# A planned graph-network kernel: transfers planned to land later, and the first filter taps and six filter steps moved ahead of the first transposition

## The chip, the cores and the metric

The kernel runs on one core of a Trainium2 chip. The metric is the device time of one execution in microseconds (us); lower is better. A core has TensorE (PE in the profile: matmuls, with the weight loads in a row of their own, PEld), VectorE (DVE), ScalarE (ACT), GpSimd (POOL) and SyncE (SP). Each works through its own queue in order. SP, ACT and POOL also issue transfers (DMAs).

## The reference

For 64 graphs of 256 nodes with 256 channels, one layer is computed: a layer norm with relu, then three branches (a convolution of width 1 and one of 17 taps along the nodes, a message step over an affinity matrix masked by the adjacency, and a gated recurrent cell that joins them), and a residual.

```python
h = jnp.maximum(_layernorm(x, axis=-1), 0.0)
xc = jnp.transpose(h, (0, 2, 1))
c = relu(bn1(conv1d(xc, conv1_w, 0)))
c = bn2(conv1d(c, conv2_w, 8))                       # 17 taps
x_conv = jnp.transpose(relu(c + xc), (0, 2, 1))
s = h @ w_se.T + b_se                                # 3 numbers a node
A = jnp.exp(-dist(s)) * adj
x_nmp = A @ relu(h @ w_msg.T + b_msg)
gi = jnp.concatenate([x_conv, x_nmp], -1) @ w_ih.T + b_ih
gh = h @ w_hh.T + b_hh
r, z = sigmoid(gi_r + gh_r), sigmoid(gi_z + gh_z)
n = tanh(gi_n + r * gh_n)
out = x + (1 - z) * n + z * h
```

## The kernel before, in words

The 64 graphs go in pairs (32 pairs, index i), and four pairs form a block (index b, 8 blocks). The 17-tap convolution is done in a transformed domain, a hand-written Fourier transform over 16 points on DVE (class Fft), so that the convolution becomes matmuls with transformed filters.

The filters are made once, at the start: `load_taps` brings the raw taps of some groups of channels (a group is 7 channels by 17 taps, 119 rows) into the tile taps, `load_points` the fixed matrices of points, and `filters` runs two matmuls aux<-taps,points or acc<-taps,points (256 columns each), one eviction by ACT (Yv<-aux, or taps<-acc where it overwrites the taps) and one transfer filt<-Yv or filt<-taps to memory. `filter_steps(n)` takes the next n of these from the list steps; they are strewn between other work, to fill TensorE. Later wb<-filt brings the filters back into the slots wb.

`norm` normalizes one pair in place: `stats` (DVE bn_stats st<-x, mv, rstd, a power on POOL), then DVE or ACT. The first four pairs lie in x, T, Sv and PT. `transpose_h` turns a pair by TensorE (aux<-ident,x) and evicts with relu into hT; `conv1` is the width-1 convolution; `split` feeds its output into V and U, the input of the transform. Before the first transposition TensorE runs WARM dummy matmuls on a zeroed tile (aux<-e).

From the second block on, a pair is turned by transfers: ACT writes hh, a transposing transfer makes halves, `sort_h` copies them back into hh, and `join_h` copies hh into hT by two ACT copies (hT<-hh). The adjacency goes the same way (`turn_adj`, `load_adj`, `join_adj`: adj<-adjh), and so does the output (`finish`, `deliver`: back<-tr, a transposing transfer gn<-back, back<-gn). x_rows holds one pair of x at a time; the next is loaded when the one before has been read by `turn_h`.

The gates of a pair are made by `seven`: a first product (acc or aux) is negated by ACT (acc<-acc) and evicted (wb<-aux), and later products are added by DVE (aux<-acc,wb and acc<-acc,wb). The sums of operand blocks that this needs are made by DVE (wb<-hT, wb<-xnm, wb<-Yv, `sums`).

The order on every engine is not that of the program. Each call is recorded as a Task, and `plan` orders the recorded tasks by a model: each engine takes, of the tasks that can start soonest, the one with the earliest late time. For TensorE late is its own running total of planned time; for a task that feeds TensorE it is worked back from there. pace is how far TensorE has come in that scale, and CALM (20 us) is the margin beyond which a task counts as not urgent. A transfer is modelled as one shared channel: self.dma is when the channel has moved it, and done, the time from which its readers can be planned, came 1.1 us later. On the chip the engines wait on semaphores, so a wrong guess of a landing costs a wait in the queue but not correctness.

`emit` is called twice. The first call comes in block 0, in front of `aggregate(0)`, and plans everything recorded by then (tasks from index 0); the second plans the rest (from a higher index), to the end. In `plan`, new is the range of the tasks that one call plans.

Of the kernel before, what the change touches and what calls it, by code (L numbers as in the profile page):

```python
# [249 lines left out]
class Recorder:  # L250
# [144 lines left out]
    def plan(self, fixed=False):  # L395

        T, new = self.tasks, range(self.planned, len(self.tasks))
        self.planned = len(T)
        total = 0.0
        for k in new:  # L400
            t = T[k]
            for p in t.preds:
                T[p].succs.append(k)
            if t.engine == "tensor":
                t.late = total
                total += t.cost
        for k in reversed(new):
            t = T[k]
            for s in t.succs:
                t.late = min(t.late, T[s].late - self.lag(t, T[s]) - self.cost(t))  # L410
            if t.first is not None:
                t.late = t.first - 1e6
        ready, free = {e: [] for e in self.LAG}, self.free
        left = {}

        def enable(k):
            at = max((T[p].done + self.lag(T[p], T[k]) for p in T[k].preds), default=0.0)
            ready[T[k].engine].append((at, k))
        for k in new:
            left[k] = sum(p in left for p in T[k].preds)  # L420
            if not left[k]:
                enable(k)
        order = []
        self.pace = 0.0

        def when(e, at, t):
            now = max(free[e], at)
            if t.size:
                now = max(now, self.lanes[e == "gpsimd"][0])
                if e != "gpsimd" and self.pace + self.CALM < t.late < math.inf:  # L430
                    now = max(now, self.dma - 1.0)
            return now

        def commit(k, e, at, now):
            t = T[k]
            ready[e].remove((at, k))
            t.begin = now
            free[e] = t.done = now + t.cost
            if e == "tensor":
                self.pace = max(self.pace, t.late)  # L440
            if t.size:
                if t.cost == self.TURN:
                    free[e] = max(free[e], self.dma + 1.1)
                self.dma = max(self.dma, now + 1.6) + t.size
                t.done = self.dma + 1.1
                lanes = self.lanes[e == "gpsimd"]
                lanes.popleft()
                lanes.append(t.done)
            order.append(k)
            for s in t.succs:  # L450
                left[s] -= 1
                if not left[s]:
                    enable(s)
        while fixed and len(order) < len(new):
            k = new[len(order)]
            e = T[k].engine
            at = next(at for at, j in ready[e] if j == k)
            commit(k, e, at, max(free[e], at, self.lanes[e == "gpsimd"][0] if T[k].size else 0.0))
        while len(order) < len(new):
            best = []  # L460
            for e in ready:
                cand = [(when(e, at, T[k]), T[k].late, k, at) for at, k in ready[e]]
                if cand:
                    now = min(cand)[0]
                    best.append((now, min(c[1:] for c in cand if c[0] <= now + 1e-9), e))
            now, (_, k, at), e = min(best)
            commit(k, e, at, now)
        return order
# [26 lines left out]
def kernel(  # L495
# [18 lines left out]
    nc = Recorder(tc.nc)  # L514
# [4 lines left out]
    PB = GB // G  # L519
    NB = B // GB  # L520
    NP = B // G
    DC = D // P
# [26 lines left out]
    def keep(name, *dims):  # L549
        return const.tile([P, *dims], FP, name=name)  # L550
# [24 lines left out]
    st, mv, rstd, shift = (Ring(keep(f"{name}{k}", *dims) for k in range(2)) for name, dims in (  # L575
        ("st", (G * MC, 6)), ("mv", (G * MC, 2)), ("rstd", (G * MC,)), ("shift", (G * MC,))))
    SLOTS = 9
    WARM = 21
    slots = [keep(f"wb{k}", DC, D) for k in range(SLOTS)]
    aux = Ring(psum.tile([P, W], FP, name=f"aux{k}") for k in range(4))  # L580
    acc = Ring(psum.tile([P, 2, W], FP, name=f"acc{k}") for k in range(2))
# [10 lines left out]
    PT, Sv, T = (Slots(t, GB * DC, L // 4, NW) for t in (PTt, Svt, Tt))  # L592
# [20 lines left out]
    def load_rows(t, src, i, eng, rows=rows):  # L613
        for g in range(G):
            eng.dma_start(out=row_tile(t, g), in_=rows(src, G * i + g))
# [4 lines left out]
    def load_x(i, eng=nc.sync):  # L620
        if i >= NP:
            return
        X[i] = SPARE[i].rearrange("p (q d) -> p q d", d=D) if i in SPARE else x_rows
        load_rows(X[i], x, i, eng, blocks if i <= PB else rows)
# [36 lines left out]
    NG = -(-P // KG)  # L661
    FULL = NG - 1
    MAIN = KG * TAPS // 16 * 16
    PARTS = [(0, FULL // 6), (FULL // 6, FULL // 3), (FULL // 3, FULL)]


    TURNS = []
# [14 lines left out]
    def load_taps(dc, a, b, eng):  # L682
        v = c2_wT[dc * P + a * KG:dc * P + b * KG].rearrange("(g k) t o -> (k t) g o", k=KG)
        for r in (slice(MAIN), slice(MAIN, KG * TAPS)):
            eng.dma_start(out=taps[r, a:b, dc, :], in_=v[r])
# [5 lines left out]
    def load_points(n, eng):  # L691
        f = bank_points[n]
        m = np.zeros((P, KG if n < len(PASSES) else LAST, f.shape[1]), np.float32)
        for k in range(m.shape[1]):
            m[k * TAPS:(k + 1) * TAPS, k] = f
        eng.dma_start(out=points[n], in_=tc.nc.inline_tensor(m.reshape(P, -1), name=f"points{n}").ap())
# [14 lines left out]
    nc.scalar.dma_start(out=w_c1, in_=c1_wT.rearrange("(k p) o -> p k o", p=P))  # L711
    load_vectors("bn1", bn1, nc.gpsimd)
    load_points(0, nc.scalar)
    for j in range(PB):
        load_x(j)
    for n in range(1, len(PASSES)):
        load_points(n, nc.sync)
    for dc in range(DC):
        load_taps(dc, *PARTS[0], nc.sync)
    load_points(len(PASSES), nc.sync)  # L720
    for part in PARTS[1:]:
        for dc in range(DC):
            load_taps(dc, *part, nc.sync)
    for dc in range(DC):
# [5 lines left out]
    p = aux()  # L730
    for _ in range(WARM):
        mm(p[:, :P], e_tile[:, 0, 0, :P], e_tile[:, 0, 0, :P], start=True, stop=True)
# [12 lines left out]
    def stats(i):  # L745

        if i >= NP:
            return
        s, m, r, h = STATS[i] = st(), mv(), rstd(), shift()
        for j in range(G * MC):  # L750
            nc.behind = BEHIND.get((i, j))
            nc.vector.bn_stats(s[:, j, :], X[i][:, j, :])
        nc.behind = None
        for j in range(G * MC):
            nc.vector.bn_aggr(m[:, j, :], s[:, j, :])
        nc.vector.tensor_scalar(r, m[:, :, 1], LN_EPS, None, ALU.add)
        if i < PB:
            BEHIND[i + 1, 0] = nc.last["vector"]
        nc.gpsimd.tensor_tensor(r, r, neg_half, ALU.pow)
        if i > PB:  # L760
            nc.vector.tensor_scalar(h, m[:, :, 0], -1.0, None, ALU.mult)
            nc.gpsimd.tensor_tensor(h, h, r, ALU.mult)
# [3 lines left out]
    def norm(i):  # L766
        stats(i)
        _, m, r, h = STATS[i]
        if i < PB:
            nc.vector.scalar_tensor_tensor(h, m[:, :, 0], -1.0, r, op0=ALU.mult, op1=ALU.mult)  # L770
        for j in range(G * MC):
            v = X[i][:, j, :]
            if i == PB or (i == 0 and j < MC):
                nc.vector.tensor_scalar(v, v, m[:, j, 0:1], r[:, j:j + 1], ALU.subtract, ALU.mult)
            else:
                nc.scalar.activation(v, v, AF.Identity, scale=r[:, j:j + 1], bias=h[:, j:j + 1])
        if i == 0:
            BEHIND[1, MC] = nc.last["vector"]
# [96 lines left out]
    def forward(k, kinds=(0, 1)):  # L875
        a = GB * DC // 2
        u, v, pt, sv, t = (s.among(k * a, (k + 1) * a) for s in (U, V, PT, Sv, T))
        if 0 in kinds:
            fft.odd(v, t, sv)
        if 1 in kinds:  # L880
            fft.even(u, pt, t)
# [413 lines left out]
            nc.gpsimd.dma_start(out=row_tile(y, g), in_=blocks(x, G * i + g), accum_op=ALU.add)  # L1295
            nc.gpsimd.dma_start(out=blocks(out, G * i + g), in_=row_tile(y, g))

    FIRST = PARTS[1][1]
    steps = deque((m, g) for g in range(FIRST) for m in range(len(PASSES)))
    steps.extend((0, g) for g in range(FIRST, FULL))  # L1300
    steps.append((len(PASSES), FULL))
    steps.extend((m, g) for m in range(1, len(PASSES)) for g in range(FIRST, FULL))
    banks = [0]

    def filter_steps(n, wide=True):
        for _ in range(n):
            banks[0] += 1
            p = acc()[:, 0] if wide and banks[0] % 3 == 0 else aux()
            filters(p, *steps.popleft(), nc.gpsimd if len(steps) % 2 else nc.sync)

    norm(0)
    power = nc.behind = nc.last["gpsimd"]
    nc.gpsimd.memset(h1, 0.0)
# [25 lines left out]
    for kind in (0, 1):  # L1339
        for k in range(2):  # L1340
            forward(k, (kind,))
    THIRD = FULL - FIRST
    filter_steps(len(steps) - THIRD - 8)
# [216 lines left out]
```

## Time and profile before

| | |
|---|---|
| median of three runs | 1669.88 us (1669.51 to 1676.13) |
| the profiled execution's own time | 1671.57 us |
| its span, first to last instruction | 1669.8 us |
| TensorE busy | 1652.6 us, 99% of the span |
| weight loads (PEld) busy | 1417.0 us, 85% |
| DVE busy | 1459.3 us, 87% |
| ACT busy | 1148.6 us, 69% |
| POOL busy | 242.5 us, 15% |
| mean granted TensorE clock | 0.997 of full speed |
| bytes moved by DMA | 261.39 MB, 157 GB/s on average |

The page sums busy time by engine. Beside it the trace gives each engine's timeline: start and duration of instructions in us, engine, output<-inputs, the shapes, the count in the row, and in brackets how long the engine had been idle and what released it. All instructions of the kernel carry the line of the helper that issues them (L378, or L374 for a joined group), so they are told apart by their tiles. A matmul in float32 shows as two records. Busy time of TensorE is modelled at its ends, so a slower stretch shows in the spacing of the starts rather than as idle time.

### The profile page before, as it was taken

The numbers are of one execution on the slowest core, as the hardware profiler recorded it, in microseconds if no ns is written. First come the engines' busy times: TensorE is split into PE (matmuls) and PEld (weight loads), VectorE is DVE, ScalarE is ACT, GpSimd is POOL, SyncE is SP. The second block draws the span as 40 slices with busy tenths as digits, with TensorE's granted clock in tenths as the row PEclk, the third lists the DMA queues.
The fourth block names the chain that finished last, engine by engine and source line by source line (L and its number), as shares of the span: only waits on it lengthen the run. The fifth ranks groups of instructions, "written<-read, shape, count | busy, mean of one in ns | idle before, by whom it ended". The sixth has DMA issues, their size and how long they took to land.

```text
span 1669.8 us, 26552 instructions
## 1 busy us (share of the span) xinstructions
PE 1652.6 (99%) x9008; PEld 1417.0 (85%) x9008; DVE 1459.3 (87%) x3391; ACT 1148.6 (69%) x2157; POOL 242.5 (15%) x245
## 2 busy tenths in 40 slices
PE   9999999999999999999999999999999999999999
PEld 6898778988899788988789887898889978898887
DVE  7979979899799997899888997989979899789645
ACT  5556676776767767686676777677676776667655
POOL 4211410013110131102110031001311013000010
PEclk9999999999999999999999999999999999999999
DMA  9982557846578455873568645784647835465022
GB/s 253 312 293 69 105 128 204 262 103 146 118 204 225 101 127 126 240 203 94 101 145 259 158 95 120 177 259 102 148 111 201 240 94 127 110 218 149 19 57 57
DMA packets 314938, 261.39 MB, mean 157 GB/s; under 512 B 192875, under 2 KB 240263, under 8 KB 314802
## 3 DMA queue, kind: packets, MB, share of 16 engines
q1 hardware_dynamic: 297010, 216.71, 49.1%
q0 software_dynamic: 17376, 42.66, 11.1%
q8 instruction: 71, 1.16, 0.3%
q14 instruction: 65, 0.53, 0.1%
q10 hardware_dynamic: 416, 0.32, 0.1%
HBM read 156.60 MB, written 43.78 MB: 120 GB/s over the span
## 4 chain that ended last, share of the span: by engine, by line
PE 79%; DVE 12%; DMA 4%; issue 2%; ACT 1%; SPq 1%; POOL 1%; ACTq 0%; DVEq 0%
PE acc L378 50%; PE aux L378 28%; DVE V L378 3%; DVE T L378 2%; DMA hh<-halves 2%; DVE Yv L378 2%; DVE wb L378 1%; DMA x<-in_x_dram 1%; PE aux L374 1%; DVE e L378 1%; SPq L378 1%; DMA wb<-filt 1%; POOL shift L378 1%; DVE msg L378 1%; DVE st L378 0%
## 5 line engine op out<-in xcount | busy, mean ns | idle before, releaser
L378 PE MATMUL acc<-wb,w_ih 128*128 128x256 f32 x768 | 189.9, 382 | 0.0
L378 PEld LDWEIGHTS acc<-wb,w_ih 128*128 128x128 f32 x768 | 146.0, 191 | 22.1 <-issue 2.3
L378 POOL DMA_DIRECT2D back<-in_x_dram x62 | 56.7, 1059 | 735.1 <-ACT back L378 594.1
L378 POOL TENSOR_TENSOR rstd<-rstd,neg_half 128x4 f32<-128x4 f32 x32 | 79.3, 2478 | 432.4 <-DVE shift L378 275.5
L378 DVE SCALAR_TENSOR_TENSOR V<-T,V 128x128 f32<-128x128 f32 (+2 forms) x448 | 141.5, 384 | 0.0
L378 ACT COPY back<-tr 128x512 uint16<-128x512 uint16 x124 | 130.4, 1078 | 15.7 <-DVE tr L378 15.3
L378 PE MATMUL aux<-wb,w_x 128*128 128x256 f32 x576 | 137.5, 381 | 2.6 <-DVE wb L378 2.6
L378 PE MATMUL acc<-wb,w_x 128*128 128x256 f32 x576 | 135.1, 380 | 0.0
L378 PEld LDWEIGHTS aux<-wb,w_x 128*128 128x128 f32 x576 | 108.7, 190 | 22.6 <-DVE wb L378 5.4
L378 PEld LDWEIGHTS acc<-wb,w_x 128*128 128x128 f32 x576 | 109.0, 190 | 18.6 <-issue 1.9
L378 PEld LDWEIGHTS acc<-U,wb 128*128 128x128 f32 x1024 | 118.3, 192 | 1.8 <-DMA wb<-filt 0.4
L378 PE MATMUL acc<-U,wb 128*128 128x128 f32 x1024 | 119.2, 275 | 0.3 <-DMA wb<-filt 0.3
L378 PE MATMUL aux<-w_msg,hT 128*128 128x259 f32 x512 | 118.6, 381 | 0.0
L378 PE MATMUL acc<-V,wb 128*128 128x128 f32 x1024 | 118.5, 275 | 0.0
L378 PEld LDWEIGHTS acc<-V,wb 128*128 128x128 f32 x1024 | 116.4, 192 | 0.5 <-DMA wb<-filt 0.5
L378 PE MATMUL acc<-wb,w_hh 128*128 128x256 f32 x384 | 105.7, 384 | 5.1 <-DVE acc L378 2.8
L378 DVE TENSOR_TENSOR e<-e,adj 128x256 f32<-128x256 f32 x128 | 68.7, 596 | 46.7 <-ACT e L378 46.7
L378 PEld LDWEIGHTS aux<-w_msg,hT 128*128 128x128 f32 x512 | 95.9, 190 | 14.1
L378 PE MATMUL aux<-hT,w_c 128*128 128x512 f32 x224 | 106.7, 600 | 0.3
L378 PE MATMUL acc<-Yv,w_ih 128*128 128x256 f32 x380 | 103.2, 381 | 2.1 <-ACT Yv L378 2.1
L378 PE MATMUL acc<-hT,w_hh 128*128 128x256 f32 x380 | 105.1, 383 | 0.0
L378 PE MATMUL acc<-xnm,w_ih 128*128 128x256 f32 x380 | 104.0, 380 | 0.0
(218 smaller groups left out, 3909.2 us busy)
## 6 DMA issues: line engine op xcount, KB each, us to landing
wb<-filt SPq DMA_DIRECT2D x348, 256.0 KB
back<-in_x_dram POOLq DMA_DIRECT2D x62, 256.0 KB, 5.3
out_dram<-back POOLq DMA_DIRECT2D x62, 256.0 KB, 3.1
x<-in_x_dram SPq DMA_DIRECT2D x58, 256.0 KB
halves_d<-halves SPq DMA_DIRECT2D x28, 512.0 KB
adjh<-halves_d SPq DMA_DIRECT2D x112, 128.0 KB
hh<-halves SPq DMA_DIRECT2D x108, 128.0 KB
filt<-Yv POOLq DMA_DIRECT2D x18, 224.0 KB, 4.3
```

What stands on the lines that cost most here:

```text
L374: self.tasks[k].call.append(lambda: method(*args, **kw))
L378: self.tasks.append(Task(engine, [lambda: method(*args, **kw)], cost, size, self.first))
```

## The change

In `plan`, `enable` sets when a task may start. A task that is not a transfer and has more than CALM to spare now gets, after each transfer that it reads, 3.0 us instead of the lag, which after a transfer is 0.0; in `commit`, a transfer's done is 2.1 us behind the channel instead of 1.1. Both are tied to new[0], the index of the first task that the call plans, being other than zero.

At the start, the first part of the taps, three groups, is split in two groups and one. The loads of the two groups stand directly behind the first pair of x, then the points, then the other three pairs of x, then the third group and the rest. The bound FIRST, the number of groups whose filter steps for all three passes come first, stays six, since its index into PARTS moves along. Six filter steps (two groups by three passes) are recorded ahead of `norm(0)`, and the dummy matmuls go from 21 to 16.

```diff
--- before.py
+++ after.py
@@ -414,7 +414,8 @@
         left = {}
 
         def enable(k):
-            at = max((T[p].done + self.lag(T[p], T[k]) for p in T[k].preds), default=0.0)
+            calm = 3.0 if new[0] and not T[k].size and self.pace + self.CALM < T[k].late < math.inf else 0.0
+            at = max((T[p].done + (calm if T[p].size else self.lag(T[p], T[k])) for p in T[k].preds), default=0.0)
             ready[T[k].engine].append((at, k))
         for k in new:
             left[k] = sum(p in left for p in T[k].preds)
@@ -442,7 +443,7 @@
                 if t.cost == self.TURN:
                     free[e] = max(free[e], self.dma + 1.1)
                 self.dma = max(self.dma, now + 1.6) + t.size
-                t.done = self.dma + 1.1
+                t.done = self.dma + (2.1 if new[0] else 1.1)
                 lanes = self.lanes[e == "gpsimd"]
                 lanes.popleft()
                 lanes.append(t.done)
@@ -575,7 +576,7 @@
     st, mv, rstd, shift = (Ring(keep(f"{name}{k}", *dims) for k in range(2)) for name, dims in (
         ("st", (G * MC, 6)), ("mv", (G * MC, 2)), ("rstd", (G * MC,)), ("shift", (G * MC,))))
     SLOTS = 9
-    WARM = 21
+    WARM = 16
     slots = [keep(f"wb{k}", DC, D) for k in range(SLOTS)]
     aux = Ring(psum.tile([P, W], FP, name=f"aux{k}") for k in range(4))
     acc = Ring(psum.tile([P, 2, W], FP, name=f"acc{k}") for k in range(2))
@@ -661,7 +662,7 @@
     NG = -(-P // KG)
     FULL = NG - 1
     MAIN = KG * TAPS // 16 * 16
-    PARTS = [(0, FULL // 6), (FULL // 6, FULL // 3), (FULL // 3, FULL)]
+    PARTS = [(0, 2), (2, FULL // 6), (FULL // 6, FULL // 3), (FULL // 3, FULL)]
 
 
     TURNS = []
@@ -711,14 +712,17 @@
     nc.scalar.dma_start(out=w_c1, in_=c1_wT.rearrange("(k p) o -> p k o", p=P))
     load_vectors("bn1", bn1, nc.gpsimd)
     load_points(0, nc.scalar)
-    for j in range(PB):
-        load_x(j)
+    load_x(0)
+    for dc in range(DC):
+        load_taps(dc, *PARTS[0], nc.sync)
     for n in range(1, len(PASSES)):
         load_points(n, nc.sync)
+    for j in range(1, PB):
+        load_x(j)
     for dc in range(DC):
-        load_taps(dc, *PARTS[0], nc.sync)
+        load_taps(dc, *PARTS[1], nc.sync)
     load_points(len(PASSES), nc.sync)
-    for part in PARTS[1:]:
+    for part in PARTS[2:]:
         for dc in range(DC):
             load_taps(dc, *part, nc.sync)
     for dc in range(DC):
@@ -1295,7 +1299,7 @@
             nc.gpsimd.dma_start(out=row_tile(y, g), in_=blocks(x, G * i + g), accum_op=ALU.add)
             nc.gpsimd.dma_start(out=blocks(out, G * i + g), in_=row_tile(y, g))
 
-    FIRST = PARTS[1][1]
+    FIRST = PARTS[2][1]
     steps = deque((m, g) for g in range(FIRST) for m in range(len(PASSES)))
     steps.extend((0, g) for g in range(FIRST, FULL))
     steps.append((len(PASSES), FULL))
@@ -1308,6 +1312,7 @@
             p = acc()[:, 0] if wide and banks[0] % 3 == 0 else aux()
             filters(p, *steps.popleft(), nc.gpsimd if len(steps) % 2 else nc.sync)
 
+    filter_steps(6)
     norm(0)
     power = nc.behind = nc.last["gpsimd"]
     nc.gpsimd.memset(h1, 0.0)
```

## The prediction

> **What bounds the kernel now.** I read the page's busy times first, then TensorE's own timeline for idle time, then the queues of ACT and DVE at each place where it stood idle, last the transfers.
>
> ```profile
> PE 1652.6 (99%) x9008; PEld 1417.0 (85%) x9008; DVE 1459.3 (87%) x3391; ACT 1148.6 (69%) x2157; POOL 242.5 (15%) x245
> ```
>
> PE is busy 99% of the span, so only three things can move the time: PE's dummy work at the start, its gaps, and the slow stretch behind a gap. The change touches no arithmetic. From PE's timeline (start, duration, what, idle before and its releaser):
>
> ```profile
> 1.85 7.73 PE L378 MATMUL aux<-e 128*128 128x128 f32 x42 [1.85 <-POOL e L378]
> 9.41 1.04 PE L378 MATMUL aux<-ident,x 128*128 128x128 f32 x8
> ...
> 208.04 0.70 PE L378 MATMUL acc<-wb,w_hh 128*128 128x256 f32 x2 [2.40 <-ACT acc L378]
> ...
> 551.07 1.13 PE L378 MATMUL aux<-wb,w_x 128*128 128x256 f32 x4 [0.52 <-DVE wb L378]
> ...
> 812.32 0.70 PE L378 MATMUL acc<-wb,w_hh 128*128 128x256 f32 x2 [1.90 <-DVE acc L378]
> 812.86 1.52 PE L378 MATMUL acc<-wb,w_ih 128*128 128x256 f32 x4
> 814.18 3.12 PE L378 MATMUL aux<-hT,w_c 128*128 128x512 f32 x4
> ...
> 1541.69 1.13 PE L378 MATMUL acc<-Yv,w_ih 128*128 128x256 f32 x4 [2.09 <-ACT Yv L378]
> ```
>
> To price a gap I take the spacing of starts in undisturbed rows: 7.77 us for 36 records is 0.216 us for 256 columns, 7.14 for 64 is 0.112 for 128 columns (each matmul has two records). Behind a long gap the spacing doubles: after 812.32 four records of 512 columns take 2.95 us to the next start where 1.72 is normal. With that, each place costs: 208: 2.4 idle, 1.8 slow, together 4.2 us. 812: 1.9 and 1.85, together 3.75. 1012: 0.8. The repeating one (551, 748, 950, 1148, 1347): 0.7, 0.45, 0.7, 0.7, 0.7, together 3.2. 1541: 4.6. 110 and 414: 1.0. Start: about 1. Sum 18.5 us, 1.1% of the span: the ceiling, apart from the dummy matmuls.
>
> Who was late? ACT ahead of 208, DVE ahead of 812:
>
> ```profile
> 199.44 1.35 ACT L378 COPY back<-gn 128x1024 uint16<-128x1024 uint16 x1 [1.60 <-DMA gn<-back]
> 202.54 1.36 ACT L378 COPY hT<-hh 128x1024 uint16<-128x1024 uint16 x1 [1.74 <-DMA hh<-halves]
> ...
> 204.90 1.34 ACT L378 COPY hT<-hh 128x1024 uint16<-128x1024 uint16 x1
> 206.09 1.34 ACT L378 COPY back<-gn 128x1024 uint16<-128x1024 uint16 x1
> ...
> 207.38 0.60 ACT L378 ACTIVATE acc<-acc 128x512 f32<-128x512 f32 x1
> ```
> ```profile
> 809.83 0.43 DVE L378 BATCH_NORM_STATS2 st<-x 128x6 f32<-128x256 f32 x1 [2.68 <-DMA x<-in_x_dram]
> ```
>
> Nothing needs these copies or statistics soon, yet they stand in an in-order queue with a transfer that is not there, and the urgent work (the negation acc<-acc; the sums wb, then acc<-acc,wb) stands behind. The order is the planner's: it believed that the transfer had landed.
>
> **What the Trainium skill says.** "TensorE: Matmul & The Clock Gate", section "What's actually happening", has PE at half clock by default and after an idle window of about 3.4 us, free-running. The trace agrees on the halving; here gaps of 1.9 to 2.4 us sufficed and those of 0.5 did not. In the first microseconds PE runs the 128-column records at 0.223 us until about 7.6 (26 of 42), then at 0.112. "DMA: Bandwidth & Descriptors", section "Issuing engines are not separate DMA queues": transfers of all queues share the same 16 engines, so order, not queue, says when the taps land; the start fits (DMA share about 1.0 from 1.8 us on). Its "Rules for kernel authors" say to issue early and wait late; the change does the second.
>
> **The change part by part.** (a) Second plan. new[0] is 0 in the first plan, so both planner edits hold only in what is recorded after the first emit, from aggregate(0), about 104 us, on. Every transfer is taken to land 1 us later, and compute with more than 20 us to spare is not enabled until 3 us after that. It adds no instruction; it reorders DVE, ACT and with them some PE. Comparing the orders place by place:
>
> At 812, 1012 and their like, st<-x moves behind the sums and the gate work, some 24 instructions later, past the late landing. The 3.75 and 0.8 should go: -4.5 us. At 414 the order stays. The moved statistics feed POOL and then hh; in this block the last three already ran at 826 to 828 and hh at 843.7, 14 us later, so the chain has that cover.
>
> At the repeating gap, hT<-hh (1.34 us twice) moves from ahead of the four exponentials to behind them, so e<-e,adj, for which DVE waited 0.67 us at 534, starts up to 1.3 us earlier, and wb<-Yv moves ahead of a transform step (0.6 us). PE needs 0.5: -3.2 us. What is late next is conv1, which needs hT: behind the exponentials ACT has the same work up to the second hT copy as it had before up to 540.34, with that copy in place of one of adj (1.33), so hT is there near 540.3, and PE starts conv1 at 542.06.
>
> At 208 ACT now does tr and wb before the copies, but hT, back, hT still stand ahead of the negation. From the landing at 202.5, three copies of about 1.24 us end at 206.25, the negation at 206.8; PE needs it at 205.6. A gap of 1.2 in place of 2.4, probably too short to halve the clock: -2.9; if it halves, -1.2. I take -2.5.
>
> Around 1541, in the last block, DVE keeps its order; this block lacks the conv1 that covers the others: 0. What the new order risks: from block 2 on it puts hT<-hh (1.34) and back<-tr (1.03) ahead of one negation that ended 0.45 us before PE's use (620.46 + 0.58, used at 621.49). DVE's two gn steps before it come about 2.3 us earlier in the new order, so I get 0 to 0.3 a block over five blocks; rounded to +1.5, between 0 and +6 (0.45 - 2.37 = -1.9 in three of them, without that help).
>
> (b) Start. WARM loses 5 matmuls, 10 records. At the full rate in which the last ones run that is 10 x 0.112 = 1.1 us; the dummies end at 8.3 in place of 9.4. Then 11 of the 12 filter matmuls (22 x 0.216 = 4.75 us) run before x's transposition, which goes from 9.41 to about 13.1. They would be run later anyway, so PE loses nothing if the taps are there. Queued ahead of them: w_c 262 KB, points 57, x 524, and taps 487, 1.33 MB. The second half of T stands at 1.37 MB before and landed at 7.5 (DVE's st<-T waited for it). I take 7.5; bounds 6.0 (bytes moved alone) and 9.5. At 9.5 PE would stand 1.2 us and may cool: +2 in all.
>
> What is moved past: on SP the T, Sv and PT pairs go behind four taps and two points (4 x 0.66 + 0.94 = 3.6 us of issue), and splitting the first part adds four taps issues (2.6 us); SP is waiting there anyway. On ACT six evictions (6 x 0.6) come before hT; on POOL three filt issues (3 x 0.55). T then lands near 10.5, its statistics, POOL's power (1.03), four ACT steps (2.1) end near 15.5; PE reaches T's transposition only near 17. DVE's transforms start 1 to 2 us later; Sv ended at 57.9 and is used at 69.6, so this is covered. Start: -1.0, between -1.6 and +2.
>
> Sum: -4.5 - 3.2 - 2.5 - 1.0 + 1.5 = -9.7 us. The profiled execution took 1671.57 us (span 1669.8), 1.69 above the median 1669.88; the difference goes onto the median: 1660.2, rounded to **1660**.
>
> **The rivals.** (1) Half of it: the gaps close but others open, since DVE is 10.0 of 10 busy in many stretches and POOL's powers vary (1.0 to 10.0 us, planned 2 to 7); POOL's waits are not in the planner's edit. Then only the DVE places are won: -4.5 - 1 + 1.5, with some of the 3.2: -4 to -8 us, about 1664. For it: ACT stood 1.96 us behind a POOL power near 792.
> (2) Slower: moved joins deliver hT too late. One place: ACT's hT<-hh before conv1 and the gates, now behind the exponentials and evictions. If it is overtaken, PE stands and cools as at 208, 4.2 us, in blocks 1 to 6: +25, less the 9.7 won: about 1685. It decides from a delay of 2 us at 542 (copies end 540) or 10 us at 837. Against it: where a transfer is really early the engine just goes on, and the copies moved by about as much as the margin or less.
> (3) The edit does nothing, because new[0] is the wrong test: excluded, since the built orders of DVE and ACT differ in every block up to the last.
> (4) Better: 208 and 1541 close as well, no new gap: -9.7 - 1.5 - 1.7 - about 3: 1654.
>
> **Numbers.** A measurement of this kernel can tell about 0.5%, 8.35 us, from no change: 1661.5. Likeliest case 0.55 (most of it below 1661.5), half of it 0.30, better 0.06, slower 0.09. Faster: 0.47 of the first, 0.03 of the second, all of the third, 0.56; same: 0.08 and 0.26, 0.34; slower 0.10 with a last 0.01 of the second. The range 1653.5 to 1668 holds (4), the first case with its bounds, and rival 1; it leaves out (2).
>
> **What would show it.** PE's idle rows: none near 812 and 1012 and none at the repeating place; about 1 us or less near 208; the one near 1541 kept. DVE's wait of st on x (12.3 us in 9) and ACT's of back on gn (16.3 in 10) much smaller. At the start 32 dummy records ending near 8.3 and a transposition near 13. I am wrong if PE waits for DMA taps at the start by over 1 us, or for ACT hT or acc at a place that recurs in each block.

## The result, and the profile after

The kernel after takes 1654.35 us (median of 4 runs, 1652.82 to 1655.23), the kernel before, run beside it, 1672.91 us (median of 4, 1669.51 to 1676.13). The ratio is 0.9888, 95% interval 0.9861 to 0.9916: the change makes the kernel 1.1% faster. The profiled executions differ by 16.6 us (1671.57 to 1654.95); the spans went from 1669.8 to 1653.2.

From the page of the kernel after, the busy times and the chain that ended last:

```profile
PE 1643.1 (99%) x8998; PEld 1415.8 (86%) x8998; DVE 1459.5 (88%) x3391; ACT 1150.7 (70%) x2157; POOL 243.6 (15%) x245
...
PE 97%; DVE 1%; DMA 1%; ACT 0%; issue 0%; POOL 0%; POOLq 0%; DVEq 0%
```

The work is the same: DVE and POOL have the same number of instructions, PE lost the ten dummy records. Its busy time fell by 9.5 us all the same. Some 1.4 us of that are the dummies (7.73 us before, 6.31 after); a stretch in which records run at half their rate counts as busy too, and by the prediction's prices those behind 208 and 812 were 3.7 us. The rest is not taken apart. In the kernel before the chain of waits ran over PE for 79% of the span and over DVE for 12%; now PE alone is 97% of it. What idle time PE has left, in PE's timeline of the kernel after (start, duration, operation, and in brackets the idle time before it and its releaser):

```profile
1.84 6.31 PE L378 MATMUL aux<-e 128*128 128x128 f32 x32 [1.84 <-POOL e L378]
7.99 2.32 PE L378 MATMUL aux<-taps,points 119*112 119x256 f32 x10
...
14.65 1.96 PE L378 MATMUL acc<-hT,w_c 128*128 128x512 f32 x4 [0.44 <-DVE rstd L378]
...
110.02 1.13 PE L378 MATMUL acc<-U,wb 128*128 128x128 f32 x8 [1.43 <-DMA wb<-filt]
...
111.47 2.94 PE L378 MATMUL acc<-U,wb 128*128 128x128 f32 x24 [0.32 <-DMA wb<-filt]
...
1525.83 1.96 PE L378 MATMUL acc<-Yv,w_ih 128*128 128x256 f32 x4 [2.09 <-ACT Yv L378]
```

Apart from the row at 7.99, which shows where the filter matmuls begin, these are all the idle rows. The places of before at 208, 414, 812, 1012 and the repeating one are closed; the one near 1541 is kept to the hundredth (now at 1525.83); the one near 110 has grown from 0.3 to 1.8 us.

To split the gain I compare the starts of one operation that comes four times in each block in the same sequence in all kernels: the joined matmuls aux<-zT. Each gap lies between two of them, and the difference of the two traces grows at:

| place (time before) | forecast, us | between the marks, us |
|---|---|---|
| start, to 87 | -1.0 | -2.25 |
| 110 | 0 | +1.28 |
| 208 | -2.5 | -3.97 |
| 414 | 0 | -0.47 |
| 812 and 1012 | -4.5 | -3.75 and -0.81 |
| repeating: 551, 748, 950, 1148, 1347 | -3.2 | -1.20, -0.55, -1.33, -1.02, -1.36 |
| 1541 | 0 | -0.56 |
| new gaps, and the rest | +1.5 | -0.44 |
| sum | -9.7 | -16.43 |

At 208 more happened than the prediction's step says. From the timelines of the kernel before, POOL and ACT (the instructions that make the shift of one pair's norm, and their reader):

```profile
176.21 1.16 POOL L378 TENSOR_TENSOR rstd<-rstd,neg_half 128x4 f32<-128x4 f32 x1 [8.04 <-DVE rstd L378]
177.46 9.98 POOL L378 TENSOR_TENSOR shift<-shift,rstd 128x4 f32<-128x4 f32 x1
...
187.47 1.58 ACT L378 ACTIVATE hh<-x,shift,rstd 128x256 f32<-128x256 f32 x3 [1.86 <-POOL shift L378]
```

The same in the kernel after, with ACT's copies and the negation that follow:

```profile
175.75 1.14 POOL L378 TENSOR_TENSOR rstd<-rstd,neg_half 128x4 f32<-128x4 f32 x1 [8.86 <-DVE rstd L378]
176.97 0.42 POOL L378 TENSOR_TENSOR shift<-shift,rstd 128x4 f32<-128x4 f32 x1
...
185.03 1.09 ACT L378 ACTIVATE hh<-x,shift,rstd 128x256 f32<-128x256 f32 x2
...
200.06 1.35 ACT L378 COPY hT<-hh 128x1024 uint16<-128x1024 uint16 x1
201.27 1.34 ACT L378 COPY back<-gn 128x1024 uint16<-128x1024 uint16 x1
202.48 1.34 ACT L378 COPY hT<-hh 128x1024 uint16<-128x1024 uint16 x1
203.69 0.62 ACT L378 ACTIVATE acc<-acc 128x512 f32<-128x512 f32 x1
```

A product of 128x4 numbers took 9.98 us before and 0.42 after. ACT no longer waits for it, so hh goes out 2.4 us earlier on the clock (1.3 us earlier in PE's terms, since PE comes to this stage 1.1 us ahead), and its copies start at 200.06 without a wait. The three copies still stand ahead of the negation, as the prediction has it; they are simply no longer late. Whether the product or the order on ACT closed the gap is what two of the experiments are for.

### The profile page after: what moved, and what is told of

Same layout as the page of the kernel before. It is cut to its first block, busy times and chain, and to the rows that moved or that the text cites. A ratio compares the mean times of both kernels' runs of the same rounds, so it can differ in the third digit from the quotient of the medians.

```text
span 1653.2 us, 26491 instructions
## 1 busy us (share of the span) xinstructions
PE 1643.1 (99%) x8998; PEld 1415.8 (86%) x8998; DVE 1459.5 (88%) x3391; ACT 1150.7 (70%) x2157; POOL 243.6 (15%) x245
## 4 chain that ended last, share of the span: by engine, by line
PE 97%; DVE 1%; DMA 1%; ACT 0%; issue 0%; POOL 0%; POOLq 0%; DVEq 0%
PE acc L378 59%; PE aux L378 37%; PE aux L374 1%; DMA wb<-filt 1%; DVE V L378 0%; DVE T L378 0%; DVE e L378 0%; DVE hh L378 0%; ACT zT L378 0%; DVE msg L378 0%; ACT Yv L378 0%; DVE wb L378 0%; ACT msg L378 0%; ACT z L378 0%; POOL e L378 0%
## 5 line engine op out<-in xcount | busy, mean ns | idle before, releaser
L378 POOL TENSOR_TENSOR rstd<-rstd,neg_half 128x4 f32<-128x4 f32 x32 | 75.6, 2364 | 402.1 <-DVE shift L378 261.5
L378 PE MATMUL aux<-e,msg 128*128 128x256 f32 x448 | 104.7, 379 | 0.0
```

The lines of the kernel that those rows point to most:

```text
L378: self.tasks.append(Task(engine, [lambda: method(*args, **kw)], cost, size, self.first))
```

## The experiments

In all of them the computation is complete. "Against after" means against the 1654.35 us, or for a place against the marks of its profiled execution. "Stage 208" is the time between the two marks around that place: 73.36 us before, 69.39 after. The kernel before, run beside each group of experiments, had medians from 1672.14 to 1675.07 us, so differences of some 2 us against after, taken between groups, say little; the ratios to before are the surer measure.

**Which half of the change does it.** The kernel before with the two planner edits alone (plan_only):

```diff
-            at = max((T[p].done + self.lag(T[p], T[k]) for p in T[k].preds), default=0.0)
+            calm = 3.0 if new[0] and not T[k].size and self.pace + self.CALM < T[k].late < math.inf else 0.0
+            at = max((T[p].done + (calm if T[p].size else self.lag(T[p], T[k])) for p in T[k].preds), default=0.0)
...
-                t.done = self.dma + 1.1
+                t.done = self.dma + (2.1 if new[0] else 1.1)
```

> The kernel before with only the two planner edits (3.0 us, 2.1 us); start, WARM and loads as before. Theory P (the second plan's order takes the late joins away from the urgent work): the gaps near 208, 812, 1012 and the repeating one are gone as in the kernel after; the two traces so far put 14.2 us of the 16.4 us behind 104 us, so about -14 us against before, near 1656. Rival S (the start shifts the phase of transfers against TensorE, and that closes the gaps): gap of 1 us or more remains near 208 or 812, at most -8 us.

Measured: 1657.10 us, ratio to before 0.9911 (0.9895 to 0.9926), so -15.0 us. PE's timeline and POOL's of this kernel:

```profile
109.73 1.13 PE L378 MATMUL acc<-U,wb 128*128 128x128 f32 x8 [0.64 <-DMA wb<-filt]
...
178.93 0.42 POOL L378 TENSOR_TENSOR shift<-shift,rstd 128x4 f32<-128x4 f32 x1
...
1527.59 1.13 PE L378 MATMUL acc<-Yv,w_ih 128*128 128x256 f32 x4 [2.09 <-ACT Yv L378]
```

Between 112 and 1527 no idle row of 0.25 us or more is left: the planner edits alone close all of them, and POOL's product takes 0.42 us.

The kernel after with the planner edits undone (start_only):

```diff
-            calm = 3.0 if new[0] and not T[k].size and self.pace + self.CALM < T[k].late < math.inf else 0.0
+            calm = 0.0 if new[0] and not T[k].size and self.pace + self.CALM < T[k].late < math.inf else 0.0
...
-                t.done = self.dma + (2.1 if new[0] else 1.1)
+                t.done = self.dma + (1.1)
```

> The kernel after with both planner edits undone; only the start part is changed (taps of two groups behind the first x, six filter steps ahead, 16 dummy matmuls). Theory P: -1 to -2.3 us against before up to 104 us, the gaps at 208, 551, 812 and so on as in before: total about -1 to -2, near 1669. Rival S: -8 us or more, with the gap near 208 or 812 gone.

Measured: 1668.63 us, ratio 0.9980 (0.9966 to 0.9994), so -3.3 us with an interval of -5.7 to -1.0; its trace is 2.34 us ahead at the first mark. From its timelines, POOL and PE:

```profile
175.70 9.98 POOL L378 TENSOR_TENSOR shift<-shift,rstd 128x4 f32<-128x4 f32 x1
...
205.68 0.70 PE L378 MATMUL acc<-wb,w_hh 128*128 128x256 f32 x2 [1.79 <-ACT acc L378]
...
546.51 1.13 PE L378 MATMUL aux<-wb,w_x 128*128 128x256 f32 x4 [0.52 <-DVE wb L378]
...
609.67 0.70 PE L378 MATMUL acc<-wb,w_hh 128*128 128x256 f32 x2 [1.17 <-DVE acc L378]
...
1007.55 0.70 PE L378 MATMUL acc<-wb,w_hh 128*128 128x256 f32 x2 [2.05 <-DVE acc L378]
1008.09 1.03 PE L378 MATMUL acc<-wb,w_ih 128*128 128x256 f32 x4
1008.95 1.88 PE L378 MATMUL aux<-hT,w_c 128*128 128x512 f32 x4
```

With the order of before the product takes 9.98 us again and the gap at 208 is there. The gaps released by DVE acc are there too, but in other blocks than in the trace of before (609 and 1007 instead of 812 and 1012): small shifts decide which block pays. No slow stretch follows the gaps of 1.79 and 2.05 us here: behind the second, four records of 512 columns take 1.72 us to the next start, where before took 2.95 behind a gap of 1.90. So stage 208 took 71.06 us in this trace, 2.30 less than before, with the same order and the same product, and part of what the places at 208 and 812 cost before is the clock and not the wait. The two halves add up: 0.9911 x 0.9980 = 0.9891, against 0.9888 for both. Rival S, that the start's shift closes the gaps, falls: the gaps stay, and the whole gains 3.3 us.

**Which of the two planner edits.** The kernel after without the 3.0 us (no_calm):

```diff
-            calm = 3.0 if new[0] and not T[k].size and self.pace + self.CALM < T[k].late < math.inf else 0.0
+            calm = 0.0 if new[0] and not T[k].size and self.pace + self.CALM < T[k].late < math.inf else 0.0
```

> The kernel after with the 3.0 us for tasks with time to spare undone (landing 1 us later kept, start kept). In its order ACT has both hT<-hh and two back<-gn ahead of the four exponentials of the repeating place. Theory P with both edits needed: the repeating gap is back or larger (5 to 7 us over the blocks), some of 208 too: +5 to +9 us against after, near 1661. Rival L (the later landing carries it all): within 2 us of after.

Measured: 1660.62 us, ratio to before 0.9934 (0.9918 to 0.9950), +6.3 against after. The kernel after with the landing at 1.1 us again (no_late):

```diff
-                t.done = self.dma + (2.1 if new[0] else 1.1)
+                t.done = self.dma + (1.1)
```

> The kernel after with the landing 1.1 us behind the channel again (the 3.0 us for tasks with time to spare kept, start kept). In its order hT<-hh stands before the four exponentials of the repeating place again, three copies stand ahead of the negation at 208. Theory P with both edits needed: the repeating gap is back (1.2 us each, 5 in all), 208 and 812 stay closed: +4 to +7 us against after, near 1660. Rival C (the 3.0 us carry it all): within 2 us of after.

Measured: 1660.64 us, ratio 0.9935 (0.9919 to 0.9952), +6.3 against after as well. The totals lie where theory P had them, but not for its reason. In both traces 414, 812, 1012 and the repeating place are closed; from 370 us to the last block neither has an idle row of 0.25 us. Most of what they lose is lost in stage 208, 75.43 us in no_calm and 74.45 in no_late. A smaller part is a place that neither before nor after has: PE waits for wb at 352 us, the repeating place's counterpart in an earlier block, 1.14 us in no_calm and 0.54 in no_late. From the timelines of no_late, POOL, ACT and PE:

```profile
175.01 9.98 POOL L378 TENSOR_TENSOR rstd<-rstd,neg_half 128x4 f32<-128x4 f32 x1 [8.98 <-DVE shift L378]
185.08 2.74 POOL L378 TENSOR_TENSOR shift<-shift,rstd 128x4 f32<-128x4 f32 x1
...
187.85 0.60 ACT L378 ACTIVATE hh<-x,shift,rstd 128x256 f32<-128x256 f32 x1 [3.25 <-POOL shift L378]
...
203.97 1.34 ACT L378 COPY hT<-hh 128x1024 uint16<-128x1024 uint16 x1 [4.88 <-DMA hh<-halves]
...
207.08 2.08 PE L378 MATMUL aux<-hT,w_c 128*128 128x512 f32 x2 [2.97 <-ACT hT L378]
```

And of no_calm, POOL, ACT and PE:

```profile
174.78 10.58 POOL L378 TENSOR_TENSOR rstd<-rstd,neg_half 128x4 f32<-128x4 f32 x1 [9.17 <-DVE shift L378]
185.44 2.74 POOL L378 TENSOR_TENSOR shift<-shift,rstd 128x4 f32<-128x4 f32 x1
...
203.96 1.34 ACT L378 COPY hT<-hh 128x1024 uint16<-128x1024 uint16 x1 [1.98 <-DMA hh<-halves]
...
207.03 1.22 PE L378 MATMUL acc<-wb,w_hh 128*128 128x256 f32 x2 [2.70 <-ACT acc L378]
```

Each chain reads upward: PE waits for ACT, ACT for the transfer of hh, hh for POOL, and POOL's two small instructions took 12.7 and 13.3 us where the kernel after needs 1.6. So for the places from 414 on either edit is nearly enough; both together were needed at 208 and, for a smaller sum, at 352. That the two edits together place the statistics of 208 where POOL gets through quickly looks like luck: nothing in the planner's model aims at it (it gives every such product the same 2.0 us).

At the repeating place the wait that was to go is gone. DVE in the block at 950, before and after:

```profile
933.31 2.13 DVE L378 TENSOR_TENSOR e<-e,adj 128x256 f32<-128x256 f32 x4 [0.81 <-ACT e L378]
```
```profile
921.37 2.12 DVE L378 TENSOR_TENSOR e<-e,adj 128x256 f32<-128x256 f32 x4
```

In no_calm and no_late ACT's exponentials stand ahead of hT<-hh in this block as well, while wb<-Yv stays behind the transform step; the two gain 0.2 us less a place than after. So of the two moves that the prediction names here, the first brings most of the gain.

**Is it POOL's product that decides at 208?** The kernel before, where for this one pair the product is made on DVE (dve_before6):

```diff
-        if i > PB:
+        if i == PB + 2:
+            nc.vector.scalar_tensor_tensor(h, m[:, :, 0], -1.0, r, op0=ALU.mult, op1=ALU.mult)
+        elif i > PB:
             nc.vector.tensor_scalar(h, m[:, :, 0], -1.0, None, ALU.mult)
             nc.gpsimd.tensor_tensor(h, h, r, ALU.mult)
```

> The kernel before, where for one pair (number 6, the first whose hh is joined near 208) the product shift = -mean x rstd is made by one DVE instruction in place of one DVE and one POOL instruction; all else as before, the orders but for some ten neighbours too. In the kernel before this POOL product took 9.98 us (177.46 to 187.44) and ACT stood 1.86 us for it ahead of hh; in the kernel after it took 0.42. Theory POOL (half or more of the gap near 208 comes from this one product): the product ends some 3 to 4 us earlier, hh lands about 1.9 earlier, the gap of 2.4 us falls below 0.7 and the slow stretch goes: -3 to -4 us by the next block. Rival A (the gap comes from ACT's order alone, three copies ahead of the negation): the gap stays, 0 to -1 us.

Measured: stage 208 takes 70.11 us in place of 73.36, -3.25, with no idle row of 0.25 us in it. The whole is 1669.77 us, ratio 0.9980 (0.9966 to 0.9994). Its timelines, PE at the start, then POOL and DVE near 180:

```profile
9.90 1.19 PE L378 MATMUL aux<-ident,x 128*128 128x128 f32 x8 [1.76 <-DVE x L378]
...
11.79 3.52 PE L378 MATMUL acc<-hT,w_c 128*128 128x512 f32 x4 [0.70 <-DVE hT L378]
...
179.44 8.44 POOL L378 TENSOR_TENSOR rstd<-rstd,neg_half 128x4 f32<-128x4 f32 x1 [8.04 <-DVE rstd L378]
...
187.91 0.16 DVE L378 SCALAR_TENSOR_TENSOR shift<-mv,rstd 128x4 f32<-128x4 f32 x1 [0.94 <-POOL rstd L378]
```

This trace runs 3.23 us behind that of before when it comes to the place, on POOL as on PE (the two rows of the start are why for 2.25 us of it, see the last section; the rest is lost near 110), so shift, ready at 188.07, is ready 2.6 us earlier in PE's terms than at 187.44 before. Now it is POOL's power that is held up, 8.44 us, but there is no product behind it. 2.6 us less on this chain close the gap with ACT's old pattern of three copies ahead of the negation. Theory POOL has it right; rival A said that the gap would stay.

The opposite: the kernel after, with POOL held up ahead of the same product (slow_shift):

```diff
             nc.gpsimd.tensor_tensor(h, h, r, ALU.mult)
+            if i == PB + 2:
+                nc.tasks[nc.last["gpsimd"]].call.insert(0, lambda: [nc.nc.gpsimd.memset(s, 0.0) for _ in range(70)])
```

> The kernel after, with 70 small memsets (128x24, on a tile no longer in use, at 0.12 us or more each) put on POOL ahead of the same product of pair 6; no other engine's order changes. Theory POOL: hh goes 1.5 to 3 us later, the gap near 208 comes back with 1 to 3 us and a slow stretch behind it: +2 to +4.5 us against after, by the next block. Rival A (the order on ACT in the kernel after, with two more evictions ahead of the copies and one copy behind the negation, covers it): within 1 us of after.

Measured: 1660.65 us, ratio to before 0.9924 (0.9901 to 0.9946), +6.3 against after; stage 208 takes 76.80 us, +7.41. Its timelines, POOL, ACT and PE:

```profile
175.91 12.19 POOL L768 MEMSET st<- 128x24 f32 x70
188.06 0.20 POOL L378 TENSOR_TENSOR shift<-shift,rstd 128x4 f32<-128x4 f32 x1
...
188.29 1.09 ACT L378 ACTIVATE hh<-x,shift,rstd 128x256 f32<-128x256 f32 x2 [4.12 <-POOL shift L378]
...
208.71 1.22 PE L378 MATMUL acc<-wb,w_hh 128*128 128x256 f32 x2 [3.92 <-ACT acc L378]
```

The memsets took 12.19 us in place of the 8.4 that I had counted on, so the loss is larger than my range; the direction and the mechanism are as theory POOL has them. ACT's new order does not cover it. With both experiments the step is settled for these two orders: in that of before an earlier end of POOL's work closes the gap, in that of after a later one opens it. It does not follow that the place of ACT's copies is without weight in other orders; calm6 below shows one that bears a late product.

**The dummies.** The kernel after with WARM = 21 (warm21):

```diff
-    WARM = 16
+    WARM = 21
```

> The kernel after with 21 dummy matmuls again; nothing else differs. If the dummies are priced rightly at the full clock: 10 records of 0.112, +1.1 us by 85 us and at the end. If the six filter steps, not the dummies, made the start's 2.3 us, 0 to +0.3.

Measured: 1654.35 us, ratio to before 0.9888 (0.9864 to 0.9913), no different from after. With WARM = 11 (warm11):

```diff
-    WARM = 16
+    WARM = 11
```

> The kernel after with 11 dummy matmuls; nothing else differs. If the taps have landed by 7.1 us (PE took the first filter matmul without a wait at 7.18 in one trace) and the clock has risen by then: -0.5 to -1.1 us. If the filter matmuls then meet the half clock or wait for taps: 0 to +1.

Measured: 1652.74 us, ratio 0.9879 (0.9852 to 0.9906), overlapping with after. The totals can't resolve five dummies, since the time at which the clock rises differs from execution to execution by more (last section). The traces can. Counting how many dummy records ran at half rate (in after 6.15 us for 32 records, so 23 of them) and bringing each trace to the same count, 26, the first mark stands at 85.31 in after and 86.43 in warm21. Five dummies are worth 1.12 us, as priced, when 21 become 16. warm11 has only 22 records, but its clock rose at nearly the same moment as in warm21 (4.9 and 5.0 us), so the two can be compared as they are: 83.97 against 85.16, 1.18 us for ten dummies. The last five thus gave less than 0.1 us at this early rise, because PE then waits for the taps; what they give at a late rise no trace here shows. In warm21, with the order of after and a product of 0.42 us, PE stands 0.61 us at 208 all the same, because ACT waits 1.06 us for the transfer of hh: the place is closed with little to spare. PE's timeline of warm11:

```profile
6.63 2.57 PE L378 MATMUL aux<-taps,points 119*112 119x256 f32 x10 [0.63 <-DMA taps<-in_c_wT_dram]
```

**Does more margin help more?** Three doses, each a change of the kernel after: the landing 3.1 us behind the channel (late31), 6.0 us for tasks with time to spare (calm6), and both edits in the first plan too (both_plans, which also sets pace to zero before the first tasks are enabled):

```diff
-                t.done = self.dma + (2.1 if new[0] else 1.1)
+                t.done = self.dma + (3.1 if new[0] else 1.1)
```

> The kernel after with the landing planned 3.1 us behind the channel in the second plan instead of 2.1. Theory P: the gaps at 414, 812, 1012 and the repeating one are already closed, so a further step wins nothing: 0 to +1 us against after, unless POOL's product near 176 meets DVE at a worse moment (10 us instead of 0.4), which costs 4 to 7 us near 208 and nothing elsewhere. Rival D (more margin helps more): -2 us or better, with the gap near 1525 smaller.

```diff
-            calm = 3.0 if new[0] and not T[k].size and self.pace + self.CALM < T[k].late < math.inf else 0.0
+            calm = 6.0 if new[0] and not T[k].size and self.pace + self.CALM < T[k].late < math.inf else 0.0
```

> The kernel after with 6.0 us instead of 3.0 for tasks with time to spare. Theory P: as for late31, 0 to +1 us, or +4 to +7 with a long POOL product near 176; also some risk of a join coming late (hT before conv1), which would show as a PE gap released by ACT hT. Rival D: -2 us or better.

```diff
+        self.pace = 0.0
...
-            calm = 3.0 if new[0] and not T[k].size and self.pace + self.CALM < T[k].late < math.inf else 0.0
+            calm = 3.0 if not T[k].size and self.pace + self.CALM < T[k].late < math.inf else 0.0
...
-                t.done = self.dma + (2.1 if new[0] else 1.1)
+                t.done = self.dma + 2.1
```

> The kernel after with both edits in the first plan as well (up to about 104 us). The first plan has no PE gap of over 0.5 us behind the start, so nothing is to be won: theory P 0 to +2 us by 87 us (transfers believed later, filter steps put behind other work), and 0 or +4 to +7 near 208, as POOL's product falls. Rival D: -1 us or better by 130 us, where PE waits 1.4 us for DMA wb.

Measured: late31 1658.32 us, ratio to before 0.9903 (0.9877 to 0.9928); calm6 1658.21, 0.9902 (0.9877 to 0.9927); both_plans 1654.52, 0.9881 (0.9856 to 0.9906). Rival D falls: no dose gains anything that can be measured. For late31 and calm6 theory P allowed 0 to +1, or a long product at 208; their medians lie some 4 us above that of after (the intervals overlap; at the last mark the traces are 3.8 and 3.4 us behind that of after), and stage 208 is not the place (69.73 and 70.16 us). In late31 the loss is spread in pieces of under 1 us: PE waits 0.15 to 0.35 us for ACT's Yv ahead of acc<-Sv,wb in each of six blocks, 0.54 us for wb at 349, and 0.48 us for acc at 1643; none of these rows is in the trace of after. In calm6 two places carry most of it, 1.4 and 1.6 us between the marks. PE's timeline:

```profile
616.01 1.13 PE L378 MATMUL acc<-wb,w_hh 128*128 128x256 f32 x4 [1.08 <-ACT acc L378]
...
1208.96 1.13 PE L378 MATMUL acc<-wb,w_hh 128*128 128x256 f32 x4 [1.32 <-ACT acc L378]
```

Ahead of the first of them ACT's timeline shows the join of another pair waiting in front of the negation:

```profile
614.00 1.35 ACT L378 COPY hT<-hh 128x1024 uint16<-128x1024 uint16 x1 [1.32 <-DMA hh<-halves]
615.38 0.58 ACT L378 ACTIVATE acc<-acc 128x512 f32<-128x512 f32 x1
```

This is the new gap that the prediction allowed for, at one dose more. In the kernel after the same hT<-hh stands ahead of this negation but its transfer is there; the negation ends at 613.98 and PE uses it at 614.56.

In calm6 POOL's two instructions took 10.8 us and in both_plans 9.1, and stage 208 lost under 1 us in both. POOL and ACT in calm6:

```profile
186.46 2.74 POOL L378 TENSOR_TENSOR shift<-shift,rstd 128x4 f32<-128x4 f32 x1
...
202.67 1.33 ACT L378 COPY hT<-hh 128x1024 uint16<-128x1024 uint16 x1
203.87 0.61 ACT L378 ACTIVATE acc<-acc 128x512 f32<-128x512 f32 x1
...
204.91 1.36 ACT L378 COPY hT<-hh 128x1024 uint16<-128x1024 uint16 x1
```

A long product alone does not make the gap: here it ends 3.1 us later in PE's terms than in before (189.20, with PE 1.35 us ahead), and PE has no idle row there. Only one hT<-hh stands ahead of the negation, the other behind it. So in another order a late product need not harm; how much of that is ACT's order and how much the transfers behind the product is not taken apart. It is in the orders of before and after that the product decides.

## Why the prediction was right, and where its steps were not

The measured 1654.35 us lies inside the range of 1653.5 to 1668, near its low end and 5.7 below the forecast of 1660; faster by over 0.5% was the likeliest outcome. That it lies inside is in part luck: the forecast starts from a median of 1669.88, and the kernel before, run beside the kernel after, took 1672.91. From there the measured gain is 18.6 us, nearly twice the forecast 9.7, and a range moved up by the same 3.0 us would have left the result out. By its steps:

- **What bounds the kernel: right; the ceiling: too low.** All of the gain that the traces show lies at PE's gaps, the slow stretches behind them and the start. The places that were said to stay (1541) and to close (812, 1012, repeating) did so. But the ceiling of 18.5 us holds 4.6 for the place at 1541, which stayed; with 1.1 for the dummies 15.0 is left, and the traces differ by 16.43. Small stalls were not in the sum. That the order of the second plan is the cause is shown: plan_only alone gives -15.0 us.
- **812 and 1012, -4.5: right**, -3.75 and -0.81 between the marks. DVE's wait of st on x fell from 12.3 us in 9 to 4.0 in 2.
- **Repeating place, -3.2: mechanism right, the term mis-sized.** Measured -5.46. I had priced the one idle row of 0.52 us and the spacing around it. In the block at 950, PE's starts show two more small stalls: the sixteen e<-msg records take 3.64 us to the next start before and 3.46 after, and two records ahead of conv1 0.69 in place of 0.43. Both are below what an idle row shows. A stall must be counted from start to start over the whole stage, not from the bracket. The wait that it named is gone, as shown above.
- **208, -2.5: the step that failed.** I took the landing of hh at 202.5 as fixed and worked out only ACT's new order behind it, with a gap of 1.2 left. Measured -3.97 and no gap. The landing itself moved, because POOL's product took 0.42 us in place of 9.98. The prediction had the number in hand and misread it: "POOL's powers vary (1.0 to 10.0 us ...)". In the trace of before the powers reach 6.8 us; the 10.0 is this product (ACT's wait near 792 was for the product too), and it stood only as a risk on the slow side. dve_before6 closes the gap by that product alone; slow_shift opens it again.
- **New gaps, +1.5: none in this kernel.** calm6 shows the named mechanism with 1.1 and 1.3 us a place, so the risk was real; the margin in the kernel after, 0.58 us at 614, was enough.
- **Start, -1.0: low.** Measured -2.25. Of that 0.3 is the clock's rise, which came earlier in this execution; of the other 1.95, 1.1 are the five dummies, as priced. The remaining 0.8 is there when the filter steps stand first (warm21 has it with 21 dummies): between the dummies and the first mark PE's small stalls, counted from start to start, sum to 2.1 us in before and 1.3 in after. The taps came earlier than the 7.5 us that I took: PE starts on them at 7.18 in no_calm without a wait, and in warm11 it waits for them until 6.63.
- **110, 0: wrong by +1.28.** PE waits there for wb<-filt, and the prediction takes that wait as unchanged. What sets the loss stays open. It is not how early PE comes: against before, the same stretch lost 0.02 us in warm11, which comes to it 3.26 us earlier, 1.58 in late31 (1.96 earlier), 0.86 in plan_only (at the same time) and 0.98 in dve_before6 (2.25 later), and won 0.48 in warm21 (2.08 earlier).
- **ACT's wait of back on gn "much smaller": wrong.** It is 17.0 us in 8, from 16.3 in 10. The waits are still there, but at 208 none stands ahead of the negation any more; the sum of a wait over the span said nothing here, its place did.

The sum came out 6.7 us short of the trace: 2.3 at the repeating place, 1.5 at 208, 1.9 on new gaps and the rest (+1.5 forecast, -0.44 measured), 1.25 at the start, 0.5 each at 414 and 1541, less 1.3 at 110. Rival 4, with 1654, had the number, but half its reason: 208 closed as well and no new gap came, while 1541 stayed. Rival 2 did not come about in this kernel.

## What to carry to other kernels

When a planner's order has idle gaps, look for urgent work queued behind a transfer that the planner thinks has landed, and give a margin only to work that has time to spare; here a small margin took nearly all, and more gave nothing or opened a gap elsewhere. Follow each late landing back to what started it, through every engine: here a product of 512 numbers on POOL held a chain of copies, and its time went from 0.42 to 9.98 us with the order of the work beside it. Price a stall from start to start over its stage, before and after, since small stalls don't show as idle rows.

## What the runs showed of the hardware

**POOL beside DVE.** The same product of 128x4 took 0.42 us (after, plan_only) and 9.98 us (before, start_only) at the same place of the program, while DVE ran instructions of 0.68 us with two inputs back to back; in no_late the power ahead of it took 9.98 us. The Trainium skill, "SBUF — State Buffer", section "SBUF: two separate sides", says that DVE with two SBUF inputs and a GpSimd instruction that reads SBUF lock a shared port pair against each other, and that the other blocks for the whole instruction. The traces agree that one holds up the other, but a hold of 9.98 us spans some sixteen DVE instructions, not one. The 70 memsets of slow_shift, which read nothing, ran beside the same run of DVE instructions at an even distance of 0.175 us with 0.11 to 0.12 us each; no hold shows there. The product's time recurs with the order: before and start_only share the order and the 9.98 us, after and plan_only theirs and the 0.42. Which DVE instruction lets POOL in is not settled.

**The clock's rise.** In 13 traced executions the dummies ran at half rate until some moment between 4.7 us (dve_before6) and 7.7 us (before, late31), where the distance of their starts falls from 0.213 to 0.112 us. The Trainium skill, "TensorE: Matmul & The Clock Gate", section "What's actually happening", puts this down to a free-running window and gives about 0.5 us either way; here the spread is 3.0 us. Brought to the same moment, the first mark lies within 0.02 us of 85.31 in seven kernels with the start of after, so the start itself repeats. An early rise doesn't always help. In dve_before6, with the start of before, it came at 4.7, the dummies ended at 8.14, PE stood 1.76 us for x and ran the next matmuls at half rate (3.52 us for four records that take 1.96). Its first mark is 2.25 us later than in before, although the clock rose 3.0 us sooner. With filter matmuls in front of the transposition PE stood at most 0.63 us ahead of them (warm11). That this is why the start's half gained 3.3 us in the median, and not only the 2.3 of its trace, is my reading and not shown. Later in the kernel a gap's length alone does not settle whether the rate halves behind it: the prediction read from the trace of before that 1.9 us suffices, but start_only ran on at the full rate behind 2.05 us.
